# A selective-scan block: convolution with two taps per matmul over shifted copies, a longer gap behind the norm's power, and the residual in the features' buffer

## The chip, the cores and the metric

The kernel runs on one core of one Trainium2 chip. The metric is device time in microseconds of one execution. The kernel before was timed three times: 4118.22, 4122.64 and 4124.35 us, median 4122.64.

## The reference

Four layers follow each other on x of 4 x 512 x 256 in fp32: a cross-attention block with a feed-forward part (layer 0), a self- and cross-attention block with a gated feed-forward part (layer 1), four selective-scan (Mamba) blocks (layer 2), and again self-attention, cross-attention and a feed-forward part (layer 3). The change lies in layer 2, whose blocks compute:

```python
def rmsnorm(x, w, eps=1e-05):
    return x * jax.lax.rsqrt(jnp.mean(x * x, axis=-1, keepdims=True) + eps) * w

def mamba_block(x, ip_w, cw, cb, xp_w, dtp_w, dtp_b, A_log, Dp, op_w):
    xz = jnp.einsum('bsd,ed->bse', x, ip_w)
    xi, z = jnp.split(xz, 2, axis=-1)
    # causal, one filter of 4 taps for each of the 512 channels
    conv = conv_general_dilated(xi.transpose(0, 2, 1), cw[:, None, :], (1,), [(3, 0)],
                                feature_group_count=512) + cb[:, None]
    xi = silu(conv.transpose(0, 2, 1))
    dt, Bm, Cm = split(einsum('bse,fe->bsf', xi, xp_w), [16, 32], axis=-1)
    dt = softplus(einsum('bsr,er->bse', dt, dtp_w) + dtp_b)
    dA = exp(dt[..., None] * -exp(A_log))
    dBu = dt[..., None] * Bm[:, :, None, :] * xi[..., None]
    # h = dA * h + dBu along the sequence, 16 states a channel; y = sum over states of h * C
    y = (ys + xi * Dp) * silu(z)
    return einsum('bse,de->bsd', y, op_w)

p = silu(prepend_cond @ pre_w1) @ pre_w2          # 64 tokens ahead of the 512
h = concatenate([p, x], axis=1)
for l in range(4):
    h = h + mamba_block(rmsnorm(h, norm_w[l]), ...)
return rmsnorm(h, final_norm_w)[:, 64:, :]
```

## The kernel before, in words

Partitions hold features in layer 2: the residual `hT` is a tile of 128 partitions x 2 chunks x 4 batches x 512 tokens that layer 1 fills at its end. The 64 prepended tokens are worked off during layers 0 and 1; they leave the scan's first states (`h63`) and the last three inputs of each convolution (`tail`).

A *unit* is one batch in one layer, 16 in all (`NU`). A unit has 512 channels as 4 blocks (`EC`) of 128 and 16 states each. Its main loop has 32 steps (`US`), 16 for each pair of channel blocks. A step scans one block over two states:

- ACT writes the two decays `exp(dt*A)` into a PSUM tile `ps_dA` (L1704; two buffers) one step ahead;
- POOL has multiplied `dBu = dtx * bB` for two steps at once (L1690), with `bB` and `bC` broadcast to all partitions by loads on SP (L1684);
- DVE scans (L1714) and multiplies by C (`hC`, L1720). For three in eight groups of two steps the scan writes into `dBu` and POOL multiplies by C instead (L1725);
- PE adds the states up by transposing them with an identity into `ps_y` (L1749). At the end of a pair DVE multiplies `ps_y` with the gate (`g`, L1765): this *closing* comes every 16 steps.

Everything else of a unit is a set of generators. Each `yield` ends one *piece*; two pieces of every running generator are issued in each step, in between the step's own instructions. The order of each engine's queue is thus written out by hand, and every engine works its queue in order.

- `front(n)` starts 16 steps into unit n-2. It squares the features on ACT (L1437), sums them on PE (`ps_r`), adds eps on DVE (L1448), and takes the power -0.5 on POOL (L1465). On the first batch of a layer it also builds on POOL, ahead of the power, the diagonal weights `w_dg` of the convolution (L1452, four operations of 128x512) and `w_dD` (L1458). Two pieces later PE broadcasts the power over the partitions (`ps_rb`, L1472) and DVE scales the features (`hn`, L1479). Then come four blocks: in-projection on PE (`ps_in`, L190), a copy by ACT to SBUF (`xp`, L1501) behind three elements that POOL copies from `tail` (L1496), the convolution as four matmuls with diagonal weights over the same `xp` shifted by 0 to 3 elements (`ps_cv`, L183), and ACT's bias (L1488). At last silu, the x-projection (`ps_x`) and the stores of B and C to `scr`, from which the broadcasts are read.
- `step` computes dt (`ps_dt`), softplus, `dtx` and the first states. `gate` computes z (`ps_z`; copies L1600). `gated` transposes g (`ps_gt`, L1618) and projects it (`ps_out`; DVE adds it to `hT`, L1633). `tokens(b)` transposes the finished features of a batch back to tokens (`ps_tk`), and applies the last norm.

All these generators share two PSUM banks, handed out by `need` and `bank`; a front has the lowest rank. Before unit 0 the front of unit 0 runs alone, with nothing beside it. Its weights (`w_inx` and others, L157) are loaded on SP as soon as the memory of layer 1 is free.

Layer 3 has its own residual `X` (`X3`), which `tokens` writes; `hT` then serves as the block-diagonal key tile `Kbd` of the cross-attention.

Of the kernel before, what the change touches and what calls it, by code (L numbers as in the profile page):

```python
# [8 lines left out]
F32 = mybir.dt.float32  # L9
# [6 lines left out]
P = 128  # L16
B = 4
T = 512
NT = B * T // P
TPB = T // P  # L20
D = 256
# [10 lines left out]
NX = R + 2 * NS  # L32
PT = B * S
# [91 lines left out]
def kernel(ctx: ExitStack, tc: tile.TileContext, t: dict, out: bass.AP):  # L125
# [1243 lines left out]
    def layer2(hT, A, far, h63, tail, X, fw, wl, late):  # L1369
# [5 lines left out]
        with ExitStack() as st:  # L1375
# [35 lines left out]
            def load_layer(l):  # L1411
                w = {
                    "x": load_w(wl, "inx", [P, DC, E], src=t["L2_in"][l][:, :E], tag="inx"),
                    "xp": load_w(wl, "xp", [P, EC, NX], src=t["L2_xp"][l], tag="xp", bufs=2),
                }
                w["dg"] = wl.tile([P, EC, 4, P], F32, name="w_dg", tag="dg")
                w["dD"] = wl.tile([P, EC, P], F32, name="w_dD", tag="dD", bufs=2)
                return w

            def load_late(l, w):  # L1420
                w["z"] = load_w(wl, "inz", [P, DC, E], src=t["L2_in"][l][:, E:], tag="inz")

# [3 lines left out]
            def front(n):  # L1426
# [23 lines left out]
                if b == 0:  # L1450
                    for m in range(EC):
                        nc.gpsimd.tensor_mul(  # L1452
                            w["dg"][:, m],
                            ident.unsqueeze(1).broadcast_to([P, 4, P]),
                            col("l2_cw", (l * EC + m) * 4, 4).unsqueeze(2).broadcast_to([P, 4, P]),
                        )
# [8 lines left out]
                nc.gpsimd.tensor_tensor(rstd, rstd, mhalf, ALU.pow)  # L1465
                yield
                yield
# [17 lines left out]
                cv = None  # L1485

                def biased(m, cv):
                    nc.scalar.activation(xi[:, m, :], cv, AF.Identity, bias=col("l2_cb", l * EC + m))  # L1488
                    done(cv)

                for m in range(EC):
                    if cv is not None:
                        biased(m - 1, cv)
                    yield from need(1, 3)
                    xp = pool.tile([P, 3 + T], F32, name="xp", tag="xp", bufs=2)
                    nc.gpsimd.tensor_copy(xp[:, 0:3], tail[:, l, b, m, :])  # L1496
                    ps = bank("in")
                    matmul_k(ps, [(w["x"][:, c, m * P : (m + 1) * P], hn[:, c, :]) for c in range(DC)])
                    yield
                    yield  # L1500
                    nc.scalar.copy(xp[:, 3:], ps)  # L1501
# [135 lines left out]
            def tokens(b):  # L1637
# [3 lines left out]
                ss = pool.tile([P, TPB], F32, name="ss", tag="rstd")  # L1641
                for j in range(0, TPB, 2):
                    yield from need(1, 1)
                    ps = bank("tk")
                    for k in range(2):
                        for c in range(DC):
                            nc.tensor.transpose(
                                ps[:, (2 * k + c) * P : (2 * k + c + 1) * P],
                                hT[:, c, b, (j + k) * P : (j + k + 1) * P],
                                ident,  # L1650
                            )
                    yield
                    yield
# [6 lines left out]
                    done(ps)  # L1660
                nc.vector.tensor_scalar(ss, ss, 1.0 / D, EPS, ALU.mult, ALU.add)
# [192 lines left out]
    def layer3(X, wa, wl):  # L1854
        with ExitStack() as st:
# [9 lines left out]
            with tc.tile_pool(name="a3s", bufs=1) as pool, tc.tile_pool(name="ps3s", bufs=1, space=PSUM) as psum:  # L1865
# [26 lines left out]
                Kbd = hT.rearrange("p c b t -> p (c b t)").rearrange("p (m b h s) -> p m b h s", m=DC, b=B, h=8)  # L1892
# [49 lines left out]
    hT = hT_pool.tile([P, DC, B, T], F32, name="hT_res")  # L1942
# [10 lines left out]
    class Beside:  # L1953


        def __init__(self, stack):
# [4 lines left out]
            store = hT.rearrange("p c b t -> p (c b t)")  # L1961
# [115 lines left out]
```

## Time and profile before

| what | us |
|---|---|
| three timed runs | 4118.22, 4122.64, 4124.35 |
| the profiled execution | 4122.01 |
| its span | 4120.0 |
| busy in the span: PE, DVE, POOL, ACT | 3508.2, 2940.4, 2343.7, 2151.2 |
| first scan (L1714) to last | 1600.3 to 3404.1 |
| scans: 304 into `ps_dA`, 208 into `dBu` | 2.29 and 2.28 each |
| `hC` (L1720), 304 | 1.22 each |
| decays (L1704), 1024 | 0.69 each |
| `dBu` products (L1690), 256; times C (L1725), 104 | 4.09 each |

The profile is one execution, shown engine by engine. "Busy" is the time in which an engine has an instruction running; PE's records of matmuls overlap, so the busy time of a group divided by its number is what one costs in a row. One fp32 matmul leaves two records. The view of waits lists, for an engine and a line, what it waited for last: total, times and longest. In a timeline a line has the start, the length, the engine, the line in the kernel, the operation and, in brackets, how long the engine stood idle before it and what released it. The page's own chain of waits covers only the end of the span, so the scan block is read from windows and timelines.

### The profile page before, as it was taken

How to read it: one execution, taken by the hardware profiler on the slowest of the kernel's cores; microseconds unless marked ns; L12 is line 12 of the kernel's file. 1: busy time of each engine (PE TensorE's matmuls, PEld its weight loads, DVE VectorE, ACT ScalarE, POOL GpSimd, SP SyncE). 2: the span in 40 equal slices, each digit the busy share in tenths (PEclk: the TensorE clock that was granted, in tenths of full speed). 3: DMA queues.
4: the chain of work that ended last, by engine and by line, in shares of the span. 5: the costliest groups of instructions: out<-in, count | busy, mean ns of one | idle time of the engine just before them, and what ended most of it. 6: DMA issues, size and time to landing. Idle time of an engine off the chain costs nothing. (4 is left out here: it accounts for less than half of the span.)

```text
span 4120.0 us, 47410 instructions
## 1 busy us (share of the span) xinstructions
PE 3508.2 (85%) x17616; PEld 2197.0 (53%) x17616; DVE 2940.4 (71%) x2821; ACT 2151.2 (52%) x4106; POOL 2343.7 (57%) x1225
## 2 busy tenths in 40 slices
PE   7989998988898897888888788888887667999889
PEld 4654554545566463555555555555555444555456
DVE  5548577576555633898989888988898996766653
ACT  2345455454212424676666666666666653556422
POOL 3349168076100425898888988898988881000131
PEclk9999999999999997988888888888888879999989
DMA  2023022033100202444444445444444441000000
GB/s 76 11 92 101 20 90 86 22 93 93 44 1 0 67 23 93 149 154 160 144 160 158 150 147 171 160 155 143 159 159 139 148 156 40 1 1 1 1 6 16
DMA packets 140486, 370.25 MB, mean 90 GB/s; under 512 B 20640, under 2 KB 38240, under 8 KB 140256
## 3 DMA queue, kind: packets, MB, share of 16 engines
q1 hardware_dynamic: 136896, 363.98, 26.8%
q10 hardware_dynamic: 3360, 3.25, 0.3%
q8 instruction: 139, 2.28, 0.2%
q14 instruction: 91, 0.75, 0.1%
HBM read 363.89 MB, written 3.28 MB: 89 GB/s over the span
## 5 line engine op out<-in xcount | busy, mean ns | idle before, releaser
L1690 POOL TENSOR_TENSOR dBu<-dtx,bB 128x2044 f32<-128x2044 f32 x256 | 1042.7, 4086 | 46.8 <-DMA bB<-scr 31.2
L1704 ACT ACTIVATE ps_dA<-dt,A 128x512 f32<-128x512 f32 x1024 | 707.8, 691 | 271.2 <-DVE hC L1720 220.8
L1714 DVE TENSOR_TENSOR_SCAN ps_dA<-ps_dA,dBu 128x1024 f32<-128x1024 f32 x304 | 696.1, 2290 | 88.3 <-ACT ps_dA L1704 88.2
L1725 POOL TENSOR_TENSOR dBu<-dBu,bC 128x2048 f32<-128x2048 f32 x104 | 425.3, 4089 | 162.3 <-issue 120.6
L1714 DVE TENSOR_TENSOR_SCAN dBu<-ps_dA,dBu 128x1024 f32<-128x1024 f32 x208 | 465.1, 2273 | 56.9 <-POOL dBu L1690 49.0
L1024 ACT ACTIVATE pr<-ps_s,nm 128x512 f32<-128x512 f32 x512 | 345.2, 686 | 259.4 <-DVE nm L1020 259.4
L1749 PE MATMUL ps_y<-ident,hC 128*128 128x128 f32 x2432 | 363.4, 299 | 92.8 <-DVE hC L1720 92.2
L1020 DVE TENSOR_REDUCE nm<-ps_s 128x2 f32<-128x1024 f32 x256 | 301.4, 1218 | 158.4 <-PE ps_s L1009 144.2
L1749 PEld LDWEIGHTS ps_y<-ident,hC 128*128 128x128 f32 x2432 | 311.6, 156 | 145.9 <-DVE hC L1720 130.1
L1720 DVE TENSOR_TENSOR hC<-ps_dA,bC 128x1024 f32<-128x1024 f32 x304 | 372.0, 1224 | 18.3 <-PE ps_y L1749 0.5
L1038 PE MATMUL ps_pt<-ident,pr 128*128 128x128 f32 x2048 | 284.9, 279 | 68.9 <-DVE pT L1043 34.7
L1038 PEld LDWEIGHTS ps_pt<-ident,pr 128*128 128x128 f32 x2048 | 232.3, 142 | 166.7 <-issue 60.4
L1749 PEld LDWEIGHTS ps_y<-ident,dBu 128*128 128x128 f32 x1664 | 233.7, 209 | 106.5 <-issue 56.8
L1749 PE MATMUL ps_y<-ident,dBu 128*128 128x128 f32 x1664 | 247.5, 294 | 45.6 <-POOL dBu L1725 45.6
L668 POOL TENSOR_TENSOR ln_rstd<-ln_rstd,const 128x4 f32<-128x4 f32 x24 | 24.4, 1018 | 444.1 <-DVE ln_rstd L667 442.5
L183 PE MATMUL ps_cv<-xp,w_dg 128*128 128x512 f32 x512 | 239.2, 602 | 37.3 <-ACT xp L1501 30.3
L587 DVE TENSOR_TENSOR_SCAN phb<-pdA,phb 128x512 f32<-128x512 f32 x128 | 224.4, 1768 | 60.9 <-POOL phb L577 44.8
L1041 ACT COPY pT<-ps_pt 128x512 f32<-128x512 f32 x256 | 140.5, 592 | 172.8 <-PE ps_pt L1038 172.3
L1057 PE MATMUL ps_o<-pT,V 128*64 128x256 f32 (+1 forms) x2048 | 222.7, 394 | 1.8 <-ACT AT L1075 1.8
L190 PE MATMUL ps_z<-w_inz,hn 128*128 128x512 f32 x256 | 150.0, 717 | 77.9 <-ACT zs L1600 49.1
L1009 PE MATMUL ps_s<-kT,qT 64*128 64x512 f32 (+1 forms) x1024 | 210.0, 648 | 2.2 <-DVE kT L1230 1.4
L577 POOL TENSOR_TENSOR phb<-hT_res,pm 128x512 f32<-128x512 f32 x128 | 187.1, 1465 | 36.6 <-DMA pm<-scrp 23.7
(275 smaller groups left out, 6287.0 us busy)
## 6 DMA issues: line engine op xcount, KB each, us to landing
bB<-scr SPq DMA_DIRECT2D x256, 512.0 KB, 3.9
bC<-scr SPq DMA_DIRECT2D x256, 512.0 KB, 4.8
pm<-scrp SPq DMA_DIRECT2D x224, 256.0 KB, 3.2
w_pw_in<-in_L_in SPq DMA_DIRECT2D x7, 512.0 KB, 4.6
X<-in_x SPq DMA_DIRECT2D x4, 512.0 KB, 7.9
w_L_W<-in_L_W SPq DMA_DIRECT2D x2, 1024.0 KB, 10.1
w_L_Wq<-in_L_Wq SPq DMA_DIRECT2D x2, 1024.0 KB, 6.3
w_L_Wo<-in_L_Wo SPq DMA_DIRECT2D x2, 1024.0 KB, 9.0
```

The source lines that it names most:

```text
L183: nc.tensor.matmul(dst, l, r, start=(i == 0), stop=(i == len(pairs) - 1))
L587: nc.vector.tensor_tensor_scan(hb, dA, hb, 0.0, ALU.mult, ALU.add)
L1020: nc.vector.tensor_reduce(nm, ps, AX.X, ALU.max, negate=True)
L1024: nc.scalar.activation(pr, ps[:, x, :], AF.Exp, bias=nm[:, x : x + 1], accum_out=rs[:, y : y + 1])
L1038: nc.tensor.transpose(pp[:, t4, :], pr[:, t4 * P : (t4 + 1) * P], ident)
L1057: nc.tensor.matmul(ps_o[0][j * stride : (j + 1) * stride, half * W2 : (half + 1) * W2], Vs[n][0][:, t4, h * stride : (h + 1) * stride], pT ...
L1690: nc.gpsimd.tensor_mul(dBus[g][:, :, 1:, :], units[n]["got", pair][1][:, 1:, :].unsqueeze(1).broadcast_to([P, 2, T - 1, 2]), bmap[g, 0][:, ...
L1704: nc.scalar.activation(dA, dt, AF.Exp, scale=A[:, l, m, s : s + 1])
L1714: nc.vector.tensor_tensor_scan(dBu if on_gpsimd(i // 2) else dA, dA, dBu, 0.0, ALU.mult, ALU.add)
L1720: nc.vector.tensor_mul(hC, dA, bmap[i // 2, 1])
L1725: nc.gpsimd.tensor_mul(h, h, bmap[g, 1].unsqueeze(3).broadcast_to([P, 2, T, 2]))
L1749: nc.tensor.matmul(y[:, j, k * P : (k + 1) * P], hC[:, s, j * P : (j + 1) * P], ident, is_transpose=True, start=False, stop=(2 * s2 + s == ...
```

## The change

In layer 2:

1. The convolution. `xp` becomes a tile of two halves of channels: half c of the channels lies on its own 64 partitions and, shifted by one element, once more on the other 64. The shifted copy is made by a DMA from SBUF to SBUF, issued on ACT. The weights `w_dg` become 128 x 64 with two taps one above the other, so that a matmul over 128 rows does two taps of 64 channels, and four matmuls do a block: two halves times two pairs of taps. ACT copies the in-projection half by half, and the three elements of `tail` too. The in-projection runs one block ahead of the convolution. `w_dg` is now one POOL operation of 128x1024, from `twos` (the two halves of the identity added) and `taps`, loaded once by four DMAs on SP.
2. Six pieces instead of two between the power and its use, from unit 2 on.
3. The residual of layer 3 lies in the buffer of `hT`. For that, `hT` is laid out batch by batch, `tokens` holds both PSUM banks and does all its transposes before it writes, and `Kbd` gets a tile of its own. The freed memory goes to a third buffer of `bB` and a fifth of `dBu`.

```diff
-                w["dg"] = wl.tile([P, EC, 4, P], F32, name="w_dg", tag="dg")
+                w["dg"] = wl.tile([P, 2, EC, 2, HP], F32, name="w_dg", tag="dg")
...
+            taps = wl.tile([P, 2, L, EC, 2], F32, name="taps")
+            at, width = _COL["l2_cw"]
+            for c in range(2):
+                for j in range(2):
+                    to = c if j == 0 else 1 - c
+                    nc.sync.dma_start(
+                        out=taps[to * HP : (to + 1) * HP, c].rearrange("p l m h -> p (l m h)"),
+                        in_=t["cols"][c * HP : (c + 1) * HP, at + j : at + width : 2],
+                    )
+            twos = wl.tile([P, HP], F32, name="twos")
+            nc.vector.tensor_add(twos, ident[:, :HP], ident[:, HP:])
...
                 if b == 0:
-                    for m in range(EC):
-                        nc.gpsimd.tensor_mul(
-                            w["dg"][:, m],
-                            ident.unsqueeze(1).broadcast_to([P, 4, P]),
-                            col("l2_cw", (l * EC + m) * 4, 4).unsqueeze(2).broadcast_to([P, 4, P]),
-                        )
-                        yield
+                    nc.gpsimd.tensor_mul(
+                        w["dg"].rearrange("p c m h e -> p c (m h) e"),
+                        twos.unsqueeze(1).unsqueeze(1).broadcast_to([P, 2, EC * 2, HP]),
+                        taps[:, :, l].rearrange("p c m h -> p c (m h)").unsqueeze(3).broadcast_to([P, 2, EC * 2, HP]),
+                    )
+                    yield
...
                 nc.gpsimd.tensor_tensor(rstd, rstd, mhalf, ALU.pow)
-                yield
-                yield
+                for _ in range(6 if n > 1 else 2):
+                    yield
...
-                for m in range(EC):
-                    if cv is not None:
-                        biased(m - 1, cv)
-                    yield from need(1, 3)
-                    xp = pool.tile([P, 3 + T], F32, name="xp", tag="xp", bufs=2)
-                    nc.gpsimd.tensor_copy(xp[:, 0:3], tail[:, l, b, m, :])
-                    ps = bank("in")
-                    matmul_k(ps, [(w["x"][:, c, m * P : (m + 1) * P], hn[:, c, :]) for c in range(DC)])
-                    yield
-                    yield
-                    nc.scalar.copy(xp[:, 3:], ps)
-                    done(ps)
-                    yield from need(1, 3)
-                    cv = bank("cv")
-                    yield from in_halves(cv, [(w["dg"][:, m, j, :], xp[:, j : j + T]) for j in range(4)])
-                    yield
-                    yield
-                biased(EC - 1, cv)
+                def projected(m):
+                    yield from need(1, 3)
+                    xp = pool.tile([P, 2, 4 + T], F32, name="xp", tag="xp", bufs=2)
+                    ps = bank("in")
+                    matmul_k(ps, [(w["x"][:, c, m * P : (m + 1) * P], hn[:, c, :]) for c in range(DC)])
+                    for c in range(2):
+                        q = slice(c * HP, (c + 1) * HP)
+                        nc.scalar.copy(xp[q, c, 0:3], tail[q, l, b, m, :])
+                    yield
+                    yield
+                    for c in range(2):
+                        q, r = slice(c * HP, (c + 1) * HP), slice((1 - c) * HP, (2 - c) * HP)
+                        nc.scalar.copy(xp[q, c, 3 : 3 + T], ps[q])
+                        nc.scalar.dma_start(out=xp[r, c, 0 : 2 + T], in_=xp[q, c, 1 : 3 + T])
+                    done(ps)
+                    return xp
+
+                xp = yield from projected(0)
+                for m in range(EC):
+                    x2 = xp
+                    if m + 1 < EC:
+                        xp = yield from projected(m + 1)
+                    else:
+                        yield
+                        yield
+                    yield from need(1, 3)
+                    cv = bank("cv")
+                    for h in range(2):
+                        for c in range(2):
+                            nc.tensor.matmul(
+                                cv[c * HP : (c + 1) * HP, :],
+                                w["dg"][:, c, m, h, :],
+                                x2[:, c, 2 * h : 2 * h + T],
+                                start=(h == 0),
+                                stop=(h == 1),
+                            )
+                    yield
+                    yield
+                    nc.scalar.activation(xi[:, m, :], cv, AF.Identity, bias=col("l2_cb", l * EC + m))
+                    done(cv)
...
-                for j in range(0, TPB, 2):
-                    yield from need(1, 1)
-                    ps = bank("tk")
+                yield from need(2, 1)
+                pss = [bank("tk") for _ in range(2)]
+                for i, ps in enumerate(pss):
...
-                tl = pool.tile([P, 2, T], F32, name=("bB", "bC")[k], tag=("bB", "bC")[k], bufs=2 + 2 * k)
+                tl = pool.tile([P, 2, T], F32, name=("bB", "bC")[k], tag=("bB", "bC")[k], bufs=3 + k)
...
-                dBus[g] = pool.tile([P, 2, T, 2], F32, name="dBu", tag="dBu", bufs=4)
+                dBus[g] = pool.tile([P, 2, T, 2], F32, name="dBu", tag="dBu", bufs=5)
...
-                Kbd = hT.rearrange("p c b t -> p (c b t)").rearrange("p (m b h s) -> p m b h s", m=DC, b=B, h=8)
+                Kbd = wp.tile([P, DC, B, 8, S], F32, name="Kbd")
...
-    hT = hT_pool.tile([P, DC, B, T], F32, name="hT_res")
+    hT_res = hT_pool.tile([P, B, DC, T], F32, name="hT_res")
+    hT = hT_res.rearrange("p b c t -> p c b t")
...
-        xp = st.enter_context(tc.tile_pool(name="X3", bufs=1))
-        X = xp.tile([P, NT, D], F32, name="X")
-        fw = row(xp, "l2_fw")
+        X = hT_res.rearrange("p b c t -> p (b c t)").rearrange("p (i d) -> p i d", d=D)
         wl = st.enter_context(tc.tile_pool(name="w2", bufs=1))
+        fw = row(wl, "l2_fw")
```

More of the change, by code (lines that the diff above doesn't have):

```diff
@@ L32 @@
 NX = R + 2 * NS
+HP = P // 2
 PT = B * S
@@ L1484, in front @@
                 xi = q["xi"] = pool.tile([P, EC, T], F32, name="xi", tag="xi", bufs=2)
-                cv = None
-                def biased(m, cv):
+                def projected(m):
[14 more added lines that the diff above has]
+                    return xp
@@ L1640, in tokens @@
                     yield
-                ss = pool.tile([P, TPB], F32, name="ss", tag="rstd")
-                for j in range(0, TPB, 2):
-                    yield from need(1, 1)
-                    ps = bank("tk")
+                ss = pool.tile([P, TPB], F32, name="ss", tag="ss")
+                yield from need(2, 1)
+                pss = [bank("tk") for _ in range(2)]
+                for i, ps in enumerate(pss):
                     for k in range(2):
+                        j = 2 * i + k
                         for c in range(DC):
                             nc.tensor.transpose(
-                                ps[:, (2 * k + c) * P : (2 * k + c + 1) * P],
-                                hT[:, c, b, (j + k) * P : (j + k + 1) * P],
-                                ident,
-                            )
-                    yield
-                    yield
+                                ps[:, (2 * k + c) * P : (2 * k + c + 1) * P], hT[:, c, b, j * P : (j + 1) * P], ident
+                            )
+                yield
+                yield
+                for i, ps in enumerate(pss):
+                    j = 2 * i
                     x = X[:, b * TPB + j : b * TPB + j + 2, :]
@@ L1660, in tokens @@
                     done(ps)
+                    yield
                 nc.vector.tensor_scalar(ss, ss, 1.0 / D, EPS, ALU.mult, ALU.add)
@@ L1960, in __init__ @@
             self.now = None
-            store = hT.rearrange("p c b t -> p (c b t)")
+            store = hT_res.rearrange("p b c t -> p (b c t)")
             self.steps = prefix_pass(
```

## The prediction

> **What bounds the kernel now.** I read the windows by stage first: of the 4120.0 us span, the scan block (layer 2) takes 1600 to 3410.
>
> ```profile
> 0.00:420.00 420.00, 365.94 (x1638) 217.78 (x1639) 245.85 (x348) 174.31 (x353) 223.24 (x203) 0.97 0.22 70
> 420.00:1600.00 1180.00, 1047.07 (x4954) 628.69 (x4953) 659.09 (x875) 472.60 (x1080) 439.17 (x343) 0.95 0.16 48
> 1600.00:3410.00 1810.00, 1465.76 (x6676) 979.04 (x6675) 1604.62 (x943) 1182.41 (x1914) 1588.51 (x578) 0.84 0.46 153
> ```
>
> Columns after the length: busy us of PE, PEld, DVE, ACT, POOL, then granted clock, DMA share, GB/s. In the third row DVE is fullest: 1604.6 of 1810. An edit here pays only as far as it shortens DVE's 205 idle us or the run-up before the first scan. Next I read whom DVE waits for between 1676 and 3412:
>
> ```profile
> DVE ps_dA L1714 <- ACT ps_dA L1704: 69.4, 85, 2.1
> DVE hT_res L1633 <- PE ps_out L183: 45.0, 15, 3.5
> DVE g L1765 <- PE ps_y L1749: 27.0, 11, 5.6
> DVE hn L1479 <- PE ps_rb L1472: 11.5, 4, 2.9
> ```
>
> So DVE waits for PE, and for ACT's decays. No POOL row is among them: POOL is off the path here. The waits of the others over the stage say why ACT and PE are late:
>
> ```profile
> ACT xi L1488 <- PE ps_cv L183: 123.0, 53, 3.9
> ...
> ACT xp L1501 <- PE ps_in L190: 59.3, 32, 6.0
> PE ps_rb L1472 <- POOL rstd L1465: 57.9, 14, 9.4
> ```
>
> ACT stands in its queue for the convolution (L1488), with the next decays behind it; PE stands for the norm's power, with the whole convolution behind it. The timeline of one layer start (unit 2, whose front also builds the weights of unit 4's layer) ties them together:
>
> ```profile
> 1915.71 2.08 PE L1472 MATMUL ps_rb<-ident,rstd 128*128 128x128 f32 x8 [9.42 <-POOL rstd L1465]
> ...
> 1932.31 3.67 PE L183 MATMUL ps_cv<-xp,w_dg 128*128 128x512 f32 x8 [1.07 <-ACT xp L1501]
> ...
> 1955.96 1.23 DVE L1765 TENSOR_TENSOR g<-ps_y,zs 128x1024 f32<-128x1024 f32 x1 [5.29 <-PE ps_y L1749]
> ```
>
> PE loses 9.4 us to the power, is then full without a gap until 1955.8, and DVE pays 2.9 at hn and 5.3 at g. Between two closings (L1765) this half unit lasts 61.7 us; the same half of units 3 and 4 takes 53.5 and 52.4, and its own DVE work is about 50 (10 steps of 2.29+1.15, 6 of 2.23, g 1.2, hn 1.4).
>
> **The change, part by part.** Lines by form give the matmul prices:
>
> ```profile
> L183 PE MATMUL ps_cv<-xp,w_dg 128*128 128x512 f32 x512 | 239.2, 602 | 37.3 <-ACT xp L1501 30.3 <-ACT dBu L1709 6.9
> ...
> L1057 PE MATMUL ps_o<-pT,V 128*64 128x256 f32 x1024 | 141.2, 398 | 1.8 <-ACT AT L1075 1.8
> ...
> L190 PE MATMUL ps_w<-w_L_Wf,gT 128*128 128x256 f32 x256 | 57.4, 379 | 0.0
> ```
>
> *Convolution on PE.* One fp32 matmul is two records: 64 blocks of 4 are 512, 239.2 us, 3.7 a block. The new block also has 4 matmuls, but each fills 64 columns and the pairs lie in different column halves. Two such tiles do overlap in layer 1: a `128*64` record of 256 columns costs 141.2/1024 = 138 ns, a full one 57.4/256 = 224, a ratio of 0.62. So 239 becomes 147, or 120 if the halves overlapped fully; I take 147, 2.3 a block. The Trainium skill ("TensorEngine Tiling (Array Packing)", Tiling Modes, Key Properties) speaks against it: changing the tiling mode drains the engine, here twice a block. The 138 against an ideal 112 already holds such drains, since layer 1 mixes the modes; by the rule's bare factor of two the sum would gain nothing more, as PE no longer sets it.
>
> What 92 us less on PE is worth is read at DVE. Two steps of a block needed 2 x 1.05 (sums, L1749) + 1.7 + 3.7 = 7.5 us of PE against 6.9 of DVE: PE fell behind. Now 6.1: it keeps up. (1) g's wait, 27.0: the last, 3.7, is the drain at the end and stays, some 1 more elsewhere: -22. (2) ACT late in the first halves after the norm (20.7 of the 69.4, summed from the timeline): I leave 6. (3) The first 22 us of the second halves, convolution tail and gate (20.6): -6. (4) Unit 0, where ACT makes DVE wait 20.4 before 1676: -4. The 45.0 for ps_out I leave whole: its PE delay starts at a z matmul that waits for ACT's zs copy (4.33 us at 1966).
>
> *Six pieces.* PE now comes to the power's result four pieces later, two steps or about 7 us; the w_dg build shrinks from four 1.04 us operations to one of twice the size (2.1) ahead of the power. 9.4 - 7 - 2.1 is nearly nothing left: hn's 11.5 go: -11.5. What is late next: the front, which has 4 pieces more here and 2 fewer in its block loop (18 for 20), ends one step later; its silu stands ten steps behind, so nobody waits.
>
> *ACT pays.* A block had one xp copy (L1501), a mean of 584 ns (0.48 from start to start where the next instruction follows at once). It now has two of half the partitions, same length; two tail copies (POOL's 64 x 0.2 us move here, 0.1 each in a row); and two DMA issues, each waiting for its copy. Issues on ACT took:
>
> ```profile
> 1991.16 0.31 ACTq L1531 DMA_DIRECT2D scr<-xd  x1
> 1991.51 0.43 ACTq L1532 DMA_DIRECT2D scr<-xd  x1
> ```
>
> 2 x (0.58 + 0.37) + 0.2 - 0.48 = 1.6 us more a block, 104 in all, ahead of the next decays, for which DVE waits. A step on DVE is 3.45 us, its decays 1.36: up to 2.1 us of lateness is free. The first block falls on two steps of 2.23 us, where 0.87 is free and the burst is 2.2: about 0.7 over, in 14 fronts: +10. The lower bound is 0; the upper bound is all 104.
>
> *The shifted copies' DMA.* 64 rows of 2 KB, like scr<-xd, which landed in 1.6 us; bC under the stage's load in 4.8. Block 0 has one step (3.5) until PE reads, the others two: 0, or 1.3 on PE x 16 without that cover. Their eight completion semaphores are shared with SP's loads, so ACT's issue sometimes also waits for a bB or bC issued three or more steps before: landed by then. The Trainium skill ("DMA: Bandwidth & Descriptors", Rules for kernel authors) speaks against two transfers to disjoint partition halves: they share the same engines and run one after the other. By it the second half would land one landing later, 3.2, and the gain at the start below would be about nothing instead of 6; no row here has two such transfers.
>
> *The start.* Before the first scan (1600.27) front 0 runs alone: convolution from 1550.71 to 1578.01, 27.3 us. With in-projection one block ahead I chain 1.7 (in), 1.9 (copies, issues), 1.6 (landing), 2.3 (conv) over two overlapping blocks and get 21.4: -6. Against it stands the tap gather: four DMAs on SP ahead of w_inx, of 64 x 32 single floats each, 8,192 pieces, 512 an engine, and w_dg, then the power, wait for them on POOL. In the changed order they wait for the last ps_f of layer 1, 1525.1 here, while
>
> ```profile
> 1541.67 4.03 POOL L1452 TENSOR_TENSOR w_dg<-ident,cols 128x512 f32<-128x512 f32 x4 [69.21 <-PE ps_tr L1310]
> ```
>
> shows when w_dg, until now without a load to wait for, started (w_inx was issued at 1541.56 and moves up with the taps: its old wait for the last transposes is gone). From 1544.0 to 1545.6, mostly w_xp's 192-byte rows, 691 packets took 74.7% of 16 engines: 28 ns each. The lone b<-scr load moved 8 packets of 64 bytes an engine in 1.0 us: 125 ns. 512 of them end, with 1.5 us of latency, at 1541 or at 1591; the power, 1547.7 before, at 1546.9 or 1594.7: -1 or +47. The gather is deep like w_xp's, not eight rows at one address; I take 40 ns: 1547.1, power 1551.2: +3.5.
>
> *Costed at nothing.* POOL loses 12.8 + 8.3 us of work and, with a third bB buffer, 31.2 us of waiting for bB: DVE does not wait for POOL, so no gain; if POOL were the bound, -52. Residual in the features' place: the final tokens take both PSUM banks at once; one more eviction in a row at the end, at most 1.5 us, and perhaps 3 us of delay in each of three fronts. A separate Kbd and the fifth dBu: no engine works longer.
>
> Sum: -22 - 14.7 + 10 - 6 - 4 - 11.5 - 6 + 3.5 = -50.7. The profiled execution took 4122.01 (span 4120.0, 2 around it), 0.6 under the median of 4122.64. So 4122.0 - 50.7 = 4071.3, **4072**.
>
> **The rivals.** *ACT becomes the bound.* Its 1.6 us a block sit ahead of the decays. For: DVE already waits for ACT 69.4 us. Against: ACT is busy 1182 of 1810 and its waits for PE fall. It decides once a block is late by more than the free 2.1 us; if DVE pays all 104 less the 10 counted, 4072 + 94 = 4166, slower. Chance 0.13. *The gather is late.* Beyond 139 ns a piece (71 us, 54 more than the 17 free) it eats the gain, at 125 ns 4072 + 43 = 4115. Chance 0.07, most of it faster or no change. *The wait only changes its name.* PE then waits for the landing of the shifted copies, ACT for PE as before, and only the power's wait and half of g's go: -11.5 - 11 + 3.5: 4103. The 4.8 us landings speak for it, the two steps against. Chance 0.18; near its upper edge no change. *More goes.* With a PE that is never behind, the gate starts on time, ps_out's 45.0 falls by two thirds: 4042. Against: its cause is ACT's zs copy. Chance 0.12.
>
> **How the numbers follow.** Forecast 0.50, own range 4052 to 4095. 4072 is the likeliest case. The range takes in the better case and part of the worse ones: 4035 to 4130; above lie about 0.15, below 0.05. A measurement here tells 0.2%, 8 us, from no change. Faster: 0.50 + 0.12 + 0.10 (renamed wait) + 0.03 (gather) = 0.75; same 0.06 + 0.02 + 0.01 (ACT) = 0.09; slower 0.02 + 0.02 + 0.12 = 0.16.
>
> **What would show it.** The ps_cv group near 147 us with `128*64` records; the wait of ps_rb for rstd under 15; g's wait under 8; layer starts at 53 instead of 61.7 us; the first scan no later than 1602; DVE's wait for ps_dA under 75. Wrong if that wait passes 110 (ACT), if ps_cv waits for xp's DMA by tens of us, if the taps land after 1560, or if ps_cv stays above 200 because the halves do not overlap.

## The result and the profile after

The changed kernel takes 4134.99 us (median of 8 runs, 4126.52 to 4138.44) against 4123.32 for the kernel before beside it: a ratio of 1.003, 95% interval 1.0019 to 1.0041. It is 12 us slower; 4072 was forecast, and the range ended at 4130. The profiled execution has a span of 4132.0 us against 4120.0.

The windows by stage, cut here at the first scan and the last closing (columns as before):

```profile
1591.00:3420.00 1829.00, 1429.03 (x6684) 940.44 (x6683) 1629.59 (x943) 1242.94 (x2094) 1573.52 (x509) 0.83 0.50 160
```

The scan block begins 9 us earlier and ends 9 us later (last closing 3420.0 against 3411.4). PE's work has shrunk; DVE's has grown by 25.0 us to 1629.6, though it was given next to nothing to do. The waits of the whole block (from the first closing on) say what became of each wait of before:

```profile
DVE ps_dA L1745 <- ACT ps_dA L1735: 82.1, 89, 3.4
PE ps_in L191 <- DVE hn L1491: 70.3, 10, 7.6
DVE hT_res L1662 <- PE ps_out L184: 41.1, 15, 3.4
...
PE ps_cv L1527 <- DMA xp<-xp: 29.4, 27, 2.2
ACT xi L1536 <- PE ps_cv L1527: 27.1, 20, 2.8
...
DVE g L1796 <- PE ps_y L1780: 20.9, 15, 3.3
...
PE ps_rb L1484 <- POOL rstd L1477: 5.8, 3, 2.5
```

PE's wait for the power (57.3 from the first closing on in the kernel before) is nearly gone, and a new one of 70.3 for `hn` stands in its place; `g` still waits 20.9 (27.0 before); ACT hardly waits for the convolution (27.1 for 118.7), and yet DVE waits for ACT's decays 82.1 (69.4). The groups by form, first the convolution, then the tokens' two small operations on DVE:

```profile
L1527 PE MATMUL ps_cv<-xp,w_dg 128*64 128x512 f32 x512 | 158.4, 610 | 33.0 <-DMA xp<-xp 30.4 <-ACT xi L1536 1.3 <-ACT dBu L1740 0.8
...
L1698 DVE SCALAR_TENSOR_TENSOR hT_res<-hT_res,ss,row_l_fw 128x256 f32<-128x256 f32 x16 | 37.1, 2375 | 1.2 <-POOL ss L1693 1.2
L1692 DVE TENSOR_SCALAR ss<-ss 128x4 f32<-128x4 f32 x4 | 8.8, 2188 | 0.0
```

In the kernel before, the scaling of the tokens was 16 of the same size for half the time, and the mean square's operation took 2.9 us for its four:

```profile
L1667 DVE SCALAR_TENSOR_TENSOR X<-X,ss,row_l_fw 128x256 f32<-128x256 f32 x16 | 19.0, 1242 | 1.2 <-POOL ss L1662 1.2
```

So these two groups grew from 21.9 to 45.9 us, nearly all of DVE's growth.

From closing to closing, summed from the timelines (us). A *first half* is here the stretch between a unit's own two closings, in which the front of two units later does its norm and its convolution; a *second half* runs from there to the next unit's first closing. A *layer start* is a first half whose front also builds the weights of a layer (units 2, 6 and 10).

| stretch | before | after | |
|---|---|---|---|
| up to the first scan | 1600.3 | 1591.4 | -8.9 |
| to the first closing | 74.9 | 69.5 | -5.4 |
| first halves, units 0 to 12 | 712.7 | 729.2 | +16.5 |
| of these the three layer starts | 185.1 | 171.6 | -13.5 |
| second halves, units 0 to 12 | 738.7 | 724.6 | -14.1 |
| last five half units, with the tokens | 284.7 | 305.5 | +20.8 |
| behind the last closing | 708.6 | 712.0 | +3.4 |

The losses are in two places: the first halves that are no layer starts (+30), and the units in which tokens are finished (+20.8). The ten waits of PE for `hn` lie one in each of the ten first halves that are no layer starts. Of the 8.9 us up to the first scan, 2.5 lie ahead of layer 2's first norm, where the change was not aimed at anything. The 3.4 us behind the last closing were not followed.

### The profile page after: what moved, and what is told of

Same layout as the page of the kernel before. It is cut to its first block, busy times and chain, and to the rows that moved or that the text cites. A ratio compares the mean times of both kernels' runs of the same rounds, so it can differ in the third digit from the quotient of the medians.

```text
span 4132.0 us, 47789 instructions
## 1 busy us (share of the span) xinstructions
PE 3470.0 (84%) x17616; PEld 2156.7 (52%) x17616; DVE 2966.5 (72%) x2822; ACT 2215.0 (54%) x4298; POOL 2324.1 (56%) x1149
## 5 line engine op out<-in xcount | busy, mean ns | idle before, releaser
L1721 POOL TENSOR_TENSOR dBu<-dtx,bB 128x2044 f32<-128x2044 f32 x256 | 1040.3, 4084 | 7.2 <-PE ps_y L1780 6.1
L1780 PE MATMUL ps_y<-ident,dBu 128*128 128x128 f32 x1664 | 259.3, 304 | 57.2 <-POOL dBu L1756 57.2
L191 PE MATMUL ps_in<-hn,w_inx 128*128 128x512 f32 x256 | 145.1, 696 | 75.7 <-DVE hn L1491 71.3
L578 POOL TENSOR_TENSOR phb<-hT_res,pm 128x512 f32<-128x512 f32 x128 | 186.8, 1462 | 34.9 <-DMA pm<-scrp 20.8
L191 PE MATMUL ps_z<-w_inz,hn 128*128 128x512 f32 x256 | 147.6, 706 | 66.9 <-ACT zs L1629 56.8
## 6 DMA issues: line engine op xcount, KB each, us to landing
xp<-xp ACTq DMA_DIRECT2D x128, 128.5 KB, 4.6
```

The costliest lines, as they stand in the source:

```text
L191: nc.tensor.matmul(dst, a, b, start=(i == 0), stop=(i == n - 1))
L1721: nc.gpsimd.tensor_mul(dBus[g][:, :, 1:, :], units[n]["got", pair][1][:, 1:, :].unsqueeze(1).broadcast_to([P, 2, T - 1, 2]), bmap[g, 0][:, ...
L1780: nc.tensor.matmul(y[:, j, k * P : (k + 1) * P], hC[:, s, j * P : (j + 1) * P], ident, is_transpose=True, start=False, stop=(2 * s2 + s == ...
```

## The experiments

Fifteen kernels, each timed beside the kernel before (4121 to 4123 us in every group). "Two pieces" is the number between the power and its use in the kernel before.

| run | kernel | us | ratio to before, 95% interval |
|---|---|---|---|
| e1 | changed, old convolution | 4190.2 | 1.015 to 1.018 |
| e2 | changed, two pieces, old buffers | 4121.0 | 0.9994 to 1.0013 |
| e3 | changed, old buffers | 4151.5 | 1.0064 to 1.0095 |
| e4 | changed, tokens' scaling off DVE | 4086.0 | 0.9903 to 0.9933 |
| e5 | before, six pieces | 4164.6 | 1.0088 to 1.012 |
| e6 | changed, two pieces | 4115.4 | 0.9975 to 0.9996 |
| e7 | e6, tokens' scaling off DVE | 4082.3 | 0.9879 to 0.9912 |
| e8 | e7, burst on ACT split | 4070.3 | 0.9856 to 0.9893 |
| e9 | before, residual's place and tokens of the change | 4137.2 | 1.0019 to 1.0048 |
| e10 | changed, GpSimd's last products halved | 4114.1 | 0.9968 to 0.9986 |
| e11 | before, tokens' scaling off DVE | 4096.9 | 0.9919 to 0.9948 |
| e12 | e8, power ahead of the tap matrices | 4076.5 | 0.9869 to 0.9899 |
| e13 | e2, burst split | 4125.1 | 0.9992 to 1.0015 |
| e14 | e2, twice the DMA issues | 4230.2 | 1.0235 to 1.0279 |
| e15 | e8, tail copies on GpSimd | 4091.1 | 0.9888 to 0.9938 |

**The parts, one at a time.** e9 has the residual's place alone, e2 adds the convolution, e3 the six pieces, the changed kernel the buffers; e1 takes the convolution out of the whole, e5 puts the six pieces alone on the kernel before, e6 takes them alone out of the changed kernel.

```
e1   the convolution's lines of the kernel before (w_dg, xp, four taps, tails on gpsimd)
e2   for _ in range(6 if n > 1 else 2): yield   ->  yield; yield
     bufs=3 + k -> 2 + 2 * k;  dBu bufs=5 -> 4
e3   only the second line of e2
e5   kernel before: yield; yield -> for _ in range(6 if n > 1 else 2): yield;  ss tag="ss"
e6   only the first line of e2
e9   e1 and e2 together
```

> The changed kernel with the old convolution (one padded row, four taps of 128 rows, tail copies on GpSimd); six pieces, buffers, residual place and tokens stay as changed. Theory (the shifted copies put a burst on ACT ahead of the decays, and this eats what PE gains): the first scan is late again by 9 us, the first halves of units 0 to 12 fall from 729 towards 713, the second halves rise from 725 towards 739, the last closings stay near 305; time 4135 within 6 either way. Rival 1 (the new convolution is a clear gain on its own and the loss is all elsewhere): 4135 + 25 = 4160 or more. Rival 2 (the new convolution is itself the loss): 4115 or less.

> The changed kernel with the power's result used two pieces later instead of six, and with two bB and four dBu buffers as before; new convolution, residual place and tokens stay. Theory: the wait of PE's ps_rb for rstd comes back at the layer starts (from 5.8 to some 30 us, less than the 57.9 of before), the three layer starts rise by 2 to 4 us each, and with the old buffers GpSimd is less dense while the last tokens are scaled, so the last closings fall from 305 to some 290; time near 4128. Rival (the tokens' lengthening comes from where they stand now, not from GpSimd's density): last closings stay at 305 and the time is 4140 or more.

> The changed kernel with two bB and four dBu buffers as before, nothing else. Theory (the tokens' scaling on DVE, from SBUF to SBUF, waits for the GpSimd instruction in flight, and the added buffers leave GpSimd no gaps): the mean of the tokens' scaling falls from 2375 ns towards the 1242 ns of before, last closings from 305 to some 288, time near 4118. Rival 1 (it is the new place of the tokens' pieces): mean stays above 2.1 us, time within 5 of 4135. Rival 2 (the buffers gain elsewhere and their loss shows): 4140 or more.

> The kernel before with six pieces instead of two between the power and its use (from the second unit's successor on), and a tag of its own for the tokens' small ss tile, nothing else. The theory of the prediction (PE no longer stands for the power, hn's wait goes): 4121 - 11.5 = 4110. Theory now (later pieces put hn and the convolution into the end of the half unit: PE then waits for hn, and g waits for the sums again): 4121 + 20 to + 35, that is 4140 to 4155; the wait of ps_rb for rstd falls below 15 in either case; PE's in-projection shows some 65 us of waiting for hn and the closings' g a wait above 40.

> The changed kernel with two pieces between the power and its use, as before; the new convolution, the third bB and fifth dBu buffer, the residual's place and the tokens as changed. Theory (the six pieces cost 30 us with the old buffers, 4151.5 against 4121.0, and the buffers gain 16.5 with six pieces, 4151.5 against 4135): both add up, 4135 - 30 = 4105; g's wait in the first halves nearly gone. Rival 1 (the buffers gain only what six pieces had lost): 4121. Rival 2 (six pieces lose only with the old buffers): 4135.

> The kernel with the residual in the features' place and the tokens that go with it, and nothing else of the change: old convolution, two pieces, two bB and four dBu buffers. Theory (the tokens' small operations on DVE stand in worse places beside GpSimd: 29.4 us of scaling in e2 with these buffers against 19.0 before, and 6 to 9 us for the mean square against 2.9): 4121 + 13 to + 17 = 4134 to 4138; then the new convolution with two pieces (e2, 4121.0) is worth some 15 us. Rival (the residual's place costs nothing): 4121, and the new convolution with two pieces is worth nothing.

e1's first rival came true: without the new convolution the changed kernel is 55 us slower, so the convolution is a gain and the loss lies elsewhere (beside two pieces and the old buffers it is worth less, see below). e3 was a miss of 33 us: the added buffers were suspected and they gain 16.5. Its mean for the tokens' scaling did fall, from 2375 to 1898 ns, but 16 times that is 7.6 us, less than the buffers bring elsewhere. The surprise is e2 against e3, which differ in the six pieces alone: 30.5 us. e5 confirms it on the kernel before, and by more than was expected (+44). e6, expected at 4105, gained 20 of the 30 us. So the steps of the way are:

| step | us | gives | first scan to last closing, profiled execution |
|---|---|---|---|
| residual's place and its tokens (before to e9) | 4123 to 4137.2 | +14.2 | +15.6 (1811.1 to 1826.8) |
| new convolution (e9 to e2) | to 4121.0 | -16.2 | -4.3 (to 1822.4) |
| six pieces (e2 to e3) | to 4151.5 | +30.5 | +24.1 (to 1846.6) |
| third bB, fifth dBu (e3 to changed) | to 4135.0 | -16.5 | -18.0 (to 1828.6) |

The last column leaves out what lies ahead of layer 2, at which no edit was aimed: in the 17 profiles layer 2's first norm starts anywhere from 1532.0 (e2) to 1543.9 us (e7), so steps of a few us are not told apart by one profile. For the convolution the run-up to the first scan comes on top (-6.1 from e9 to e2), so some 10 of its 16 us are to be seen in layer 2.

In another order the prices differ (six pieces: +44 on the kernel before, +30.5 here, +19.6 from e6 to the changed kernel, +3.7 from e7 to e4); the steps are not independent, and a median from four to ten runs can be a few us off. e5's tag for `ss` costs nothing: its last five half units, where the tokens are, take 283.3 us for 284.7.

*How the six pieces lose.* The timeline of one first half (unit 5, from closing to closing), the kernel before:

```profile
2232.37 1.20 DVE L1765 TENSOR_TENSOR g<-ps_y,zs 128x1024 f32<-128x1024 f32 x1
...
2240.01 2.08 PE L1472 MATMUL ps_rb<-ident,rstd 128*128 128x128 f32 x8 [2.92 <-POOL rstd L1465]
...
2246.07 1.38 DVE L1479 SCALAR_TENSOR_TENSOR hn<-hT_res,cols,ps_rb 128x512 f32<-128x512 f32 x2
2248.40 1.88 PE L190 MATMUL ps_in<-hn,w_inx 128*128 128x512 f32 x4
2275.18 3.60 PE L183 MATMUL ps_cv<-xp,w_dg 128*128 128x512 f32 x8
2284.58 1.22 DVE L1765 TENSOR_TENSOR g<-ps_y,zs 128x1024 f32<-128x1024 f32 x1 [0.95 <-PE ps_y L1749]
```

The same half in e5:

```profile
2248.65 1.20 DVE L1765 TENSOR_TENSOR g<-ps_y,zs 128x1024 f32<-128x1024 f32 x1
...
2260.17 1.13 PE L1472 MATMUL ps_rb<-ident,rstd 128*128 128x128 f32 x8
...
2267.99 1.38 DVE L1479 SCALAR_TENSOR_TENSOR hn<-hT_res,cols,ps_rb 128x512 f32<-128x512 f32 x2
2268.86 3.62 PE L190 MATMUL ps_in<-hn,w_inx 128*128 128x512 f32 x4 [7.57 <-DVE hn L1479]
2301.97 1.99 PE L183 MATMUL ps_cv<-xp,w_dg 128*128 128x512 f32 x4
2307.08 1.22 DVE L1765 TENSOR_TENSOR g<-ps_y,zs 128x1024 f32<-128x1024 f32 x1 [5.95 <-PE ps_y L1749]
```

The 2.92 us for the power are gone. But `hn` is written on DVE, in DVE's order of steps, three pieces behind the broadcast: 13.7 us after the closing in the kernel before, 19.3 in e5. PE, no longer late, comes to the in-projection and stands 7.57 us for `hn`. All four blocks then run later, the last convolution ends 55.3 us after the closing instead of 46.4, on top of the last sums, and `g` waits 5.95 instead of 0.95. Over the block e5 has `g` waiting 64.1 us and PE 76.9 for `hn`. The in-projection that comes out of the long stand is slow besides: 3.62 us for four records, 1.88 in the kernel before. Its granted clock was 0.51 (2268.9 to 2272.3) against 1.00 there (2248.4 to 2250.2). In the kernel before the wait of 2.92 us had been followed by a clock of 0.50 too, but it fell on the small broadcast (2.08 us, 1.13 in e5). All ten waits of the changed kernel for `hn` have an in-projection of 3.4 to 3.75 us behind them.

**The tokens on DVE.** e4, e7 and e11 take the two-SBUF-operand work off DVE; e10 leaves it there and cuts GpSimd's instructions.

```
-  nc.vector.tensor_copy(x.rearrange("p a d -> p (a d)"), ps)
+  nc.vector.tensor_mul(x, ps.rearrange(...), fw.unsqueeze(1).broadcast_to([P, 2, D]))
-  nc.vector.tensor_scalar(ss, ss, 1.0 / D, EPS, ALU.mult, ALU.add)
+  nc.gpsimd.tensor_scalar(ss, ss, 1.0 / D, EPS, ALU.mult, ALU.add)
-  nc.vector.scalar_tensor_tensor(X[:, i, :], X[:, i, :], ss[:, j : j + 1], fw, ALU.mult, ALU.mult)
+  nc.scalar.activation(X[:, i, :], X[:, i, :], AF.Identity, scale=ss[:, j : j + 1])
e10  last layer: dBu<-dtx,bB and dBu<-dBu,bC once for each of the two states, half the size
```

> The changed kernel; the final tokens are multiplied by the weight row while they are evicted from PSUM on DVE, the norm's factor is applied on ACT, and the mean square's scaling goes to GpSimd: DVE keeps no SBUF-to-SBUF operation of the tokens. Theory (those operations cost DVE 37 + 9 us in the changed kernel, 24 more than before): last closings fall from 305 to some 262 to 270 and the time to 4092 to 4102, below the kernel before. Rival (their length overlapped other waits, or ACT's 16 new instructions make the decays late by as much): last closings above 290, time above 4118.

> The changed kernel with two pieces and with the tokens' scaling taken off DVE (weight row in the eviction, norm's factor on ACT, mean square on GpSimd). If the two effects add: 4105 - 49 = 4056. Rival (with two pieces the tokens meet fewer GpSimd instructions, so their price is smaller): 4075.

> The changed kernel with each of GpSimd's long products of the last layer (dBu from dtx and bB, dBu times bC; 4.1 us each) cut into two instructions of half the size. Theory (each scaling of a token on DVE waits for one GpSimd instruction in flight): its mean falls from 2375 ns to about 1300, the mean square's from 2188 to about 1200, the last closings fall by some 20 us, time near 4116. Rival 1 (DVE waits for GpSimd's queue or for the shared memory's bandwidth, whatever the length of one instruction): mean stays within 10 per cent of 2375 and the time within 6 of 4135. Rival 2 (shorter instructions cost GpSimd more in all and it becomes late): above 4141.

> The kernel before with only the tokens' scaling taken off DVE's two SBUF operands (weight row in the eviction, norm's factor on ACT, mean square on GpSimd). Theory (DVE pays 19.0 + 2.9 us for them there): 4121 - 20 = 4101. Rival (in that kernel they overlap waits that DVE has anyway): above 4115.

e4 gains 49 us on the changed kernel (46 us had stood there), e11 26 on the kernel before (22), e10 21. e7 was a miss: the gains of e4 and e6 should have added to 4056 to 4066, and it took 4082.3. The timeline of DVE and GpSimd in the changed kernel, behind unit 13:

```profile
3134.94 4.06 POOL L1721 TENSOR_TENSOR dBu<-dtx,bB 128x2044 f32<-128x2044 f32 x1
3135.05 3.97 DVE L1692 TENSOR_SCALAR ss<-ss 128x4 f32<-128x4 f32 x1
...
3145.76 13.08 DVE L1698 SCALAR_TENSOR_TENSOR hT_res<-hT_res,ss,row_l_fw 128x256 f32<-128x256 f32 x4
3145.97 4.18 POOL L1756 TENSOR_TENSOR dBu<-dBu,bC 128x2048 f32<-128x2048 f32 x1 [1.75 <-issue]
3150.12 8.44 POOL L1721 TENSOR_TENSOR dBu<-dtx,bB 128x2044 f32<-128x2044 f32 x2
```

An operation on 128x4 takes 3.97 us and ends with the GpSimd product that it fell upon; four scalings end with the third product in a row. At the kernel's end, with GpSimd idle, the same four take 1.67 us:

```profile
3434.74 1.67 DVE L1698 SCALAR_TENSOR_TENSOR hT_res<-hT_res,ss,row_l_fw 128x256 f32<-128x256 f32 x4 [1.18 <-POOL ss L1693]
```

In e10, with GpSimd's instructions at 2147 ns instead of 4084, the groups are:

```profile
L1698 DVE SCALAR_TENSOR_TENSOR hT_res<-hT_res,ss,row_l_fw 128x256 f32<-128x256 f32 x16 | 25.4, 1645 | 1.2 <-POOL ss L1693 1.2
L1692 DVE TENSOR_SCALAR ss<-ss 128x4 f32<-128x4 f32 x4 | 4.7, 1184 | 0.0
```

The wait shrinks with the length of the GpSimd instruction: without the four at the end, 12 scalings take (25.4 - 1.67) / 12 = 1.98 us each there, 2.95 in the changed kernel. So DVE waits for the instruction in flight, and the "busy" time of such a group is mostly waiting. That is also what the residual's place costs: in e9 the scaling takes 29.4 us and the mean square 7.4 (19.0 and 2.9 before), 14.9 more, against 14.2 in the kernel's time. An eviction of 512 columns from PSUM, between the same products, took 0.69 us in both kernels. The Trainium skill ("SBUF — State Buffer", Who interferes with whom) says that a DVE instruction with two SBUF inputs contends with a GpSimd instruction that reads SBUF, and that their shared port pair is an exclusive lock; the rows of the scaling agree. The mean square's operation has one SBUF input and waited like them.

**The burst on ACT.** e8 and e13 put a piece of the front between a block's two half copies; e14 doubles the issues; e15 moves the tail copies. e12 belongs to the layer starts.

```
e8, e13   for c in range(2):
              if c and n > 1: yield
e14       each xp<-xp in two DMAs of half the columns
e15       nc.scalar.copy(xp[q, c, 0:3], ...) -> nc.gpsimd.tensor_copy
e12       rstd's pow moved ahead of the w_dg and w_dD products
```

> The run e7 with one more piece of the front between the two half copies of a block, from the second unit's successor on, so that at most one copy and one DMA issue stand ahead of a step's decays. Theory (the burst of two copies and two issues makes the decays late by 1.3 to 2 us twice in a first half): DVE's waits for ACT's decays in the first halves fall by about 2 us a unit in 14 units, some 25 us less than e7, 4030. Rival 1 (the lateness has other causes, or the burst is paid anyway in two parts): within 6 of e7. Rival 2 (the longer front ends later and what follows is late): above e7 by 10 or more.

> The run e2 (new convolution, two pieces, old buffers) with one more piece of the front between the two half copies of a block. Theory (the burst makes the decays late): DVE's waits for ACT (117 us in e2) fall by 20 or more, as between e7 and e8 (115 to 86); part comes back as g's wait (e7 to e8: 7 to 29); time 4121 - 10 = 4111. Rival (the waits come from elsewhere, so the split moves nothing): waits within 8 of 117, time within 6 of 4121.

> The run e2 with each shifted copy sent in two DMAs of half the columns: two more issues of some 0.47 us a block in the same burst, 128 issues and 60 us of ACT's queue in all, the copies as before. Theory (the burst stands on the path once a step's free 2.1 us are used up): DVE's waits for ACT rise by a third to two thirds of that, 20 to 40 us, and the time to 4140 to 4160. Rival (issues hide, the copies' engine time makes the lateness): waits within 8 of 117, time within 8 of 4121.

> The run e8 with the two small tail copies of a block back on GpSimd as in the kernel before (128 copies of half the partitions, some 0.2 us each there). Theory (they are ahead of the decays on ACT, 0.1 to 0.2 us a block): time between 4060 and 4070. Rival (ACT's big copy, which writes the same tile, now waits for GpSimd's copy behind a product of 4.1 us): 4080 or more.

> The run e8 with the norm's power issued on GpSimd ahead of the tap matrices at a layer start instead of behind them (two pieces as before). Theory (what was left of PE's wait for the power at layer starts, 10 waits of up to 2.9 us and 29 us in all with the layer starts the longest, needed an earlier power and not a later use): ps_rb's wait for rstd falls below 20, the layer starts lose 1 to 2 us each, time 4062 to 4067. Rival (the tap matrices are then late for the convolution): 4075 or more.

The timeline of ACT in e2, one block:

```profile
2240.47 0.58 ACT L1510 COPY xp<-ps_in 64x512 f32<-64x512 f32 x1
2241.08 0.47 ACTq L1511 DMA_DIRECT2D xp<-xp  x1
2241.59 0.58 ACT L1510 COPY xp<-ps_in 64x512 f32<-64x512 f32 x1 [0.54 <-ACT xp L1510]
2242.20 0.47 ACTq L1511 DMA_DIRECT2D xp<-xp  x1
2242.72 1.42 ACT L1735 ACTIVATE ps_dA<-dt,A 128x512 f32<-128x512 f32 x2 [0.55 <-ACT xp L1510]
```

2.25 us pass between the block's first copy and the next decays. Splitting does what it should to the decays: DVE's waits for ACT (both scan forms, from 1600 us on) fall from 117.4 to 96.0 us (e2 to e13) and from 114.9 to 86.0 (e7 to e8). But the four extra pieces move the front back, and `g` waits again: 4.9 to 34.9 and 7.2 to 28.9. e13 gains nothing, e8 12 of the 25 us expected. e14 fell worse than its theory: +109 us for 128 more issues, more than their whole length. DVE's waits for ACT rise by as much, from 117.4 to 225.0 us, and ACT also stands in its queue:

```profile
2294.00 0.58 ACT L1510 COPY xp<-ps_in 64x512 f32<-64x512 f32 x1
2298.41 1.14 ACTq L1512 DMA_DIRECT2D xp<-xp  x2
2299.59 0.58 ACT L1510 COPY xp<-ps_in 64x512 f32<-64x512 f32 x1 [5.02 <-issue]
```

The copy ends at 2294.58, the issue begins 3.83 us later, and the half unit has a DVE wait of 6.5 us there. The trace's semaphores say what the issue waited for. ACT's copies share eight completion semaphores with SP's loads, and the one that this issue needs was last used by a load of bB:

```profile
2294.15 0.32 SPq L1716 DMA_DIRECT2D bB<-scr  x1
```

It landed at 2298.34; ACT's wait ended at 2298.36. In e14 ACT's queue stands like this for a bB or bC load 19 times, 55.4 us in all, 15 of them for bB, about one a front; in e2 three times, at the layer starts, 7.2 us; in the changed kernel never. So e14 does not price the issues alone, and it can't tell its theory (the burst) from these landings. e15 is a miss: GpSimd's small copies stand behind products of 4.1 us (ACT waits 24.6 us for them), 21 us slower than e8. e12 is not told apart from e8: the wait for the power stays at 29.1 us, because it is ten waits of 2.9 in the first halves that are no layer starts, where e12's edit does not act; its expectation had put the longest of them at the layer starts.

## Why the prediction was wrong

By the steps of the sum:

| step | predicted | measured |
|---|---|---|
| convolution (all its terms, gather and start included) | -39.2 | -16.2 (e9 to e2) |
| six pieces | -11.5 | +30.5 (e2 to e3) |
| residual's place, tokens | 0 | +14.2 (before to e9) |
| buffers | 0 | -16.5 (e3 to changed) |
| sum | -50.7 | +12.0 |

**The step that failed is "Six pieces"**, 42 of the 63 us: "nearly nothing left: hn's 11.5 go", and "the front ... ends one step later; its silu stands ten steps behind, so nobody waits". The wait for the power did go (57.3 to 5.8), and hn's 11.5 with it: in the changed kernel `hn` no longer waits for the broadcast. What was said to be late next was the end of the front alone. What was late was each thing inside it: `hn` on DVE 5.6 us later in e5, with PE behind it (70.3 us of a new wait in the changed kernel), and the four blocks pushed into the closing. The step also took the layer start, with its 9.4 us, for all fronts. The row of hn's 11.5 us counts four waits, three of them layer starts and one in unit 0; in the other first halves DVE did not wait, PE's wait for the power was 2.9 us, and four pieces, "about 7 us", were more than it. There the new wait stands: layer starts fell by 13.5 us, the other first halves rose by 30.

**"Costed at nothing" was wrong twice.** The tokens' operations were said to make no engine work longer. They cost 14.2 us in their new places beside GpSimd (e9), and the added buffers make GpSimd run without gaps (its products' wait for bB is 31.2 us before, about 1 after), which took the scaling from 1898 to 2375 ns. The buffers' own gain (16.5 with six pieces, 5.6 with two) was denied because DVE does not wait for GpSimd by name. That reading took DVE's busy time for work: in the tokens' groups it is waiting for GpSimd, and e11 takes 26 us out of it on the kernel before. e2 to e6 shows the buffers' gain in the second halves, 738.2 to 725.2 us, and up to the first closing, 76.0 to 69.7; by what chain was not followed.

**The convolution was right in kind and mis-sized.** Its PE time came out as worked (158.4 for 147; 309 ns a record instead of 467). The `g` term holds: 27.0 to 4.9 in e2. The start holds: from the first norm's square to the first scan 58.7 us became 52.3, -6.4 for -6. The taps were there at 1531, 12 us before the power, so the gather's +3.5 was 0 and its upper bound far off. The rule on two transfers to disjoint halves that the prediction weighed was not put to the test: at the start the issues are 1.16 us apart, the first transfer's packets moved from about 1552.8 to 1553.7 us and the second's from 1553.9 to 1554.8, one after the other, and each landed 2.2 us after its own issue. The landing of 3.2 that would have cost the gain did not come. Elsewhere the copies were mis-sized: they are of 128.5 KB, twice the scr<-xd whose 1.6 us the prediction took, and they landed with a median of 4.6 us; PE's 29.4 us for them had been put at 0. The ACT terms failed: -14.7 and +10 were to leave 4.7 less; in e2 DVE's waits for ACT (both scan forms, from 1600 us on) rise from 96.1 to 117.4. A block cost ACT not 1.6 but some 2.2 us more (2.25 + 0.4 - 0.48), and it hit three of the four blocks of a first half, not the first alone: in unit 5 of e2 DVE waits 1.8, 1.3, 0.3 and 0.7 in a row. So from e9 to e2 the three layer starts gain 14.2 us (186.8 to 172.6) and the other first halves lose 12.5 (528.1 to 540.6). Unit 0's -4 did not come from the convolution (75.0 us to the first closing in e9, 76.0 in e2; the later 69.5 came with the buffers), and the second halves gained nothing from it (737.5 to 738.2). A small misreading decides nothing: in the half unit said to be "full without a gap" PE has two gaps, 0.89 and 1.07 us.

**The signs.** ps_cv, ps_rb, the first scan and the taps went as forecast. `g` (20.9, not under 8), the layer starts (56.8 to 57.9, not 53) and ps_dA (82.1, not under 75) did not. PE's wait for xp's landing, 29.4 us, was among the signs of being wrong; e2 with 40.0 us of it is no slower than the kernel before, so it decides little here. Of the rivals, "the wait only changes its name" was nearest in kind, but named the wrong wait (the landing, not `hn`). None had more pieces as a loss.

**What stays open.** Why the six pieces cost less the more of the rest is in place (+44 to +3.7), how much of their loss is the lower clock behind the stand, and by what chain the buffers gain.

**A faster version.** e8, the changed kernel with two pieces, the weight row multiplied in at the tokens' eviction and the burst split, takes 4070.3 us, ratio 0.9875 (0.9856 to 0.9893). e11 shows that about half of it is to be had without the change at all.

## What to carry to other kernels

A wait that is removed by issuing its consumer later moves everything behind the consumer as well: list each engine that the later work passes through, and what it then collides with at the end of the period. An operation's duration is no property of the operation: if its group's mean is several times its length alone, look for another engine's instruction that ends at the same time. A short burst ahead of a paced stream costs by the step in which it lands, so price it at every landing, not at the first.

## What the hardware showed that was not expected

A DVE operation on 128x4 in SBUF took 3.97 us beside a GpSimd product of 4.06 us and 0.16 us with GpSimd idle. With products back to back, a scaling of 128x256 took 2.95 us beside products of 4.1 us and 1.98 beside products of 2.15, 0.42 with GpSimd idle. Four DMAs of 2,048 single floats each took 6.29 us to issue on SP and had landed within 9.3 us of the first issue. After a stand of 7.57 us PE's next four records took 3.62 us at a granted clock of 0.51, instead of 1.88 at 1.00. 128 more DMA issues on ACT cost 109 us, though an issue lasts about half a microsecond; 55 us of ACT's queue went to waits for loads issued on another queue, which shared the copies' completion semaphores.
